# Keys of the context: from GpSimd operations to DMAs, in a two-layer cross-attention block

## The chip, the core and the metric

The kernel runs on one core of a Trainium2 chip. Its engines are TensorE (PE; PEld is its weight load), VectorE (DVE), ScalarE (ACT), GpSimd (POOL) and SyncE (SP, which here only issues DMAs). The metric is the device time of one execution in microseconds; the time before is 3352.13 us, the median of three runs (3349.53 to 3354.31).

## The reference

Two transformer blocks in float32, one after the other, over `x` of 4 x 512 x 320 and a context of 4 x 1601 x 192. There are 20 heads of 16.

```python
def _attn(x, ctx, wq, wk, wv, wo, bo, heads):
    q = (x @ wq).reshape(b, n, heads, dh).transpose(0, 2, 1, 3)
    k = (ctx @ wk).reshape(b, j, heads, dh).transpose(0, 2, 1, 3)
    v = (ctx @ wv).reshape(b, j, heads, dh).transpose(0, 2, 1, 3)
    a = softmax(einsum('bhid,bhjd->bhij', q, k) * dh ** -0.5)
    return einsum('bhij,bhjd->bhid', a, v).transpose(0, 2, 1, 3).reshape(b, n, -1) @ wo + bo
...
x = _attn(ln(x), ln(x), ...) + x            # self-attention
x = _attn(ln(x), context, ...) + x          # cross-attention, 1601 keys
a, g = split(ln(x) @ ff_w1 + ff_b1)
x = (a * gelu(g)) @ ff_w2 + ff_b2 + x       # feed-forward, 1280 wide
```

## The kernel before

**Units.** A layer is a list of units. A self-attention or cross-attention unit is one batch element and one group of four heads: 4 x 5 = 20 of each kind in a layer. A feed-forward unit is one batch element. Over two layers there are 40 cross units. A unit works through its keys in chunks of 128: 4 chunks in self-attention, 13 in cross-attention (12 full ones and a tail of 65 keys).

**What one chunk step does** (`main`, from L987). PE makes the scores of the chunk transposed, keys by queries, one matmul a head (`st`, L995). ACT takes their exponentials into `pr` (L1001). One step later PE multiplies these by the values of the four heads (`av`, L1015). Except for the first chunk, ACT copies that product to `vo` (L1031) and GpSimd adds it to the unit's sum `o` (L1032). `pr` and `vo` come from one ring of eight buffers (`prs`, L93, tag `pr`). Beside this, PE makes the scores of a coming unit a first time (`sps`, L835 and, for the tail, L849) and DVE takes their row maxima (`pm` and `nmax`, L843): the negated maximum goes into a row of the query tile by eight small DMAs (`max_end`, L885 to L899: `q<-turned`) three chunks before a unit ends, so that the score matmul subtracts it.

**Slots.** TensorE's rows are used in four slots of 32, a head in each. A head has 16 rows of keys, so half a slot is left: one row of it holds ones in the key tile, against the row of maxima in the query tile, and the others zeros. `HEAD` says which head a slot takes: slots 0 and 1 hold heads 0 and 2 in their lower 16 rows, slots 2 and 3 heads 1 and 3 in their upper 16. `keep` and `ones` are columns that mask the rows that a slot keeps and add its ones. The three key tiles `kT` (`kbuf`, L124) hold 128 rows by 1601 keys. Self units use `kbuf[0]`, three units beside each other; cross units use all three in turn. The feed-forward uses columns of `kbuf[1]` and `kbuf[2]` for its hidden values.

**Keys of the context** (`keys_of_context`, L687 to L721). The context stands transposed in four quarters of the array's rows, so each of four PSUM banks `a` takes a quarter of the keys, and in it each half `i` of the quarter has 64 rows: four heads of 16. The matmuls (L697) are 192 columns wide, with up to 32 more in half 1 for the tail, `more = [32, 32, 1, 0]`. ACT and DVE copy two banks each to a stage tile `kst` (L707), the columns of the tail by copies of their own (L709). Then eight closures (`piece`) are put on the unit's `kslots`; each calls `to_slots` (L572 to L587), which writes 64 rows of keys to both halves of the slots on GpSimd, two operations a piece for 192 keys and two more where there are tail columns:

```python
nc.gpsimd.tensor_scalar(to, stage[rows, :w], keep[b][rows], more[rows], ALU.mult, ALU.add)
```

Queries and the keys of self-attention go to their slots by the same line.

**What sets the order.** The instructions of each engine and each queue run in the order in which this program issues them. That order is planned while the program is built. There are chains of jobs (`divide`, `project`, `slots`, `norm`, `context`, `early`, `proj`, `values`), each job with a cost and a due round. `steps` (L360) runs once in a chunk step and takes the jobs with the nearest due round, as far as a credit allows; two rounds pass in a chunk step. Pieces cost 0.0, and `clock["slots"]` bounds them to two a step. When the last piece of a unit is issued, `there()` notes the round, and the first scores of that unit (`sps`) wait three rounds more (`at_hand`, L1201), unless they are due at once (`at_once`, L1205).

**Queues.** Nearly all DMAs go by SP, in the program's order: `q<-turned`, four `aT<-o` a unit that gather the finished output of a group (`turn` in `add_finish`, L926 to L934), the context loads (`load_context`, L492; two in flight, the next one issued by the job that has turned the last but one, which waits until three rounds after its load), weights, and the result. Weight loads wait in the list `loads`; one entry is issued in each attention unit, three chunks before its end. The rows behind the last tokens of the context, in its last tile of 128, are cleared by a memset on GpSimd (L503).

**Other work of GpSimd**: the residual's bias add (L465), part of the inverse root of the norms (L399 to L406), and the queries' slots.

Of the kernel before, what the change touches and what calls it, by code (L numbers as in the profile page):

```python
# [9 lines left out]
F32 = mybir.dt.float32  # L10
I32 = mybir.dt.int32
AF = mybir.ActivationFunctionType
ALU = mybir.AluOpType
# [4 lines left out]
S2, CTX = 1601, 192  # L18
H, DH = 20, 16
# [3 lines left out]
P = 128  # L23
NQ = N // P
G, HG = 5, 4
# [40 lines left out]
def kernel(ctx: ExitStack, tc: tile.TileContext, x, context, ws, out):  # L66
# [54 lines left out]
        nmax.append(m)  # L121


    kbuf = [const.tile([P, S2], F32, name=f"kT{i}") for i in range(3)]  # L124
    qbuf = [const.tile([P, N], F32, name=f"q{i}") for i in range(4)]
    fill = qbuf[3]
    nc.vector.memset(fill, 1.0)

    kept = []
    for b in range(2):  # L130
# [229 lines left out]
    def steps(beside, lights=1):  # L360


        tick()
        clock["lights"], clock["slots"] = lights, 2
        clock["tiles"] = True if beside is None else None
        done = 0
        while True:
            name = pick()
            if name is None:
                break  # L370
            cost = sum(chains[name][0][0])
            if cost >= 0.1:
                share = (0.5, 3.0) if beside else (9.0, 9.0) if beside is False else (0.5, 0.75, 1.5)
                least = cost * share[done] if done < len(share) else 3.0
                if clock["credit"] < (3.0 if beside is False else least):
                    break
                done += 1
                if clock["tiles"] is not None:
                    clock["tiles"] = name in ALIKE
            run(name)  # L380
            if cost == LIGHT:
                clock["lights"] -= 1
            clock["slots"] -= name == "slots"
        clock["tiles"] = None
# [107 lines left out]
    def load_context(b, i):  # L492
        c0, n = CGRP[i]
        t = two.tile([P, 2, CTX], F32, tag="ctxin", name="ctxin")
        rows = min(S2, (c0 + n) * P) - c0 * P
        full = rows // P
        if full:
            dma(
                out=t[:, :full, :],
                in_=context[b, c0 * P : (c0 + full) * P, :].rearrange("(c p) d -> p c d", p=P),  # L500
            )
        if rows % P:
            nc.gpsimd.memset(t[rows % P // SLOT * SLOT :, full, :], 0.0)  # L503
            dma(out=t[: rows % P, full, :], in_=context[b, (c0 + full) * P : S2, :])
        ctx_in[b, i] = t, clock["round"]

# [4 lines left out]
    def add_context(l, b, put, due, free):  # L511
        s = {}

        def tiles():
            s["cT"] = one.tile([P, KB, QT + 32], F32, tag="ctxT", name="ctxT")
            s["tail"] = one.tile([CK[0][2], 2, TAIL], F32, tag="tail", name="tail")

        def load():
            tiles()
            dma(out=s["cT"], in_=saved[b])  # L520
            dma(out=s["tail"], in_=saved_tail[b])
            s["round"] = clock["round"]

        if l:
            add("context", 0.0, load, due - 14, free)
            add("context", 0.0, lambda: put(s), due - 2, yes, lambda: clock["round"] >= s["round"] + 8)
            return

        def turn(i):
            if i == 0:  # L530
                tiles()
            c0, n = CGRP[i]
            t, _ = ctx_in.pop((b, i))
            for c in range(n):
                at = (c0 + c) * 32
                nc.vector.transpose(s["cT"][:, :, at : at + 32], t[:, c, :])
            if i + 2 < len(CGRP):
                load_context(b, i + 2)
            if i + 1 == len(CGRP):
                dma(out=saved[b], in_=s["cT"])  # L540
                s["last"] = t

        def tail():
            ps = step_bank([P, 2, P], "cps")
            for k, at, w in CK:
                nc.tensor.transpose(ps[:w, k, :TAIL], s["last"][:TAIL, 0, at : at + w], ident[:TAIL, :TAIL])
            w = CK[0][2]
            nc.scalar.copy(s["tail"], ps[:w, :, :TAIL])
            dma(out=saved_tail[b], in_=s["tail"])
            put(s)  # L550

        for i in range(len(CGRP)):
            add(
                "context", LIGHT, lambda i=i: turn(i), due - 2 * (len(CGRP) - i), free if i == 0 else yes,
                lambda i=i: clock["round"] >= ctx_in[b, i][1] + 3,
            )
        add("context", 0.3, tail, due)

# [13 lines left out]
    def to_slots(t, c0, stage, w, i, with_ones, direct=None):  # L572

        rows = slice(i * GD, (i + 1) * GD)
        for b in range(2):
            to = t[b * GD : (b + 1) * GD, c0 : c0 + w]
            more = ones[b] if with_ones else zero
            if direct:

                if b:  # L580
                    nc.vector.tensor_scalar(to, stage[rows, :w], direct[b][rows], more[rows], ALU.mult, ALU.add)
                else:
                    nc.scalar.activation(
                        to, stage[rows, :w], AF.Identity, bias=more[rows], scale=direct[b][rows]
                    )
                continue
            nc.gpsimd.tensor_scalar(to, stage[rows, :w], keep[b][rows], more[rows], ALU.mult, ALU.add)  # L587

    def add_proj(u):
# [97 lines left out]
        def keys_of_context():  # L687

            pss = quarter_banks("kps")

            more = [max(0, min(32, TAIL - a * 32)) for a in range(4)]
            for k in range(KB):
                for a, ps in enumerate(pss):
                    rows = slice(a * SLOT, (a + 1) * SLOT)
                    for i in range(2):
                        w = HALF + i * more[a]
                        nc.tensor.matmul(  # L697
                            ps[i * GD : (i + 1) * GD, :w],
                            lhsT=wk_q[rows, k, u.g * GD : (u.g + 1) * GD],
                            rhs=first.kvT[rows, k, i * HALF : i * HALF + w],  # L700
                            start=(k == 0),
                            stop=(k == KB - 1),
                        )
            stage = one.tile([P, 4, HALF + 32], F32, tag="kstage", name="kst4")
            for a, ps in enumerate(pss):
                copy = nc.vector.tensor_copy if a % 2 else nc.scalar.copy
                copy(stage[:, a, :HALF], ps[:, :HALF])  # L707
                if more[a]:
                    copy(stage[GD:, a, HALF : HALF + more[a]], ps[GD:, HALF : HALF + more[a]])  # L709
            for a in range(4):  # L710
                for i in range(2):
                    def piece(a=a, i=i):
                        to_slots(u.kT, a * QT + i * HALF, stage[:, a, :], HALF, i, True)
                        if i and more[a]:
                            to_slots(u.kT, 4 * QT + a * 32, stage[:, a, HALF:], more[a], i, True)
                        if a == 3 and i:
                            there()

                    u.kslots.append(piece)
            u.keyed = True  # L720
            first.made["kv"] += 1  # L721

# [14 lines left out]
        if not u.cross:  # L737
            add_queries()
            add(chain, (0.477,) * 3, keys, due, free)
        else:  # L740
            add(chain, 2.45, keys_of_context, keys_due, free)
            add_queries()
            for i in range(8):
                add(
                    "slots", 0.0, lambda: u.kslots and u.kslots.popleft()(), keys_due,
                    lambda: u.keyed, lambda: clock["slots"] > 0,
                )
# [434 lines left out]
    def after(u):  # L1182

        stage[u.b] += 1
        if u.b == B - 1:
            load_bias(u.l, ("self", "cross", "ff").index(u.kind) + 2)
            if u.kind == "self":
                loads.append(lambda: load_out(u.l, "o2_w"))
            if u.kind == "cross" and u.l + 1 < L:
                loads.append(lambda: load_out(u.l + 1, "o1_w"))  # L1190
            if u.l + 1 < L:
                if u.kind == "ff":
                    loads.append(lambda: load_cross(u.l + 1))
                    load_ff(u.l + 1)
                elif u.kind == "self":
                    loads.append(lambda: load_self(u.l + 1))
# [65 lines left out]
    load_bias(0, 0)  # L1262
    load_bias(0, 1)


    add_norms(0)
    add_proj(units[0])
    warm(5)
# [14 lines left out]
    max_reduce(first)  # L1283
    max_end(first)
    load_x(1)
    loads.append(lambda: load_x(2))
    loads.append(lambda: load_out(0, "o1_w"))
    loads.append(lambda: load_x(3))
    loads.append(lambda: load_cross(0))
# [51 lines left out]
```

## Time and profile before

| | |
|---|---|
| median of three runs | 3352.13 us |
| the profiled execution's own time | 3352.16 us |
| its span | 3350.4 us |
| mean granted clock of TensorE | 0.988 |
| L587, keys and queries to slots on GpSimd | 1036 + 476 operations |
| SP's DMAs on the hardware queue | 52416 packets, 52.15 MB |

The profile is one execution on the chip. Its span runs from the first to the last instruction. A row of a group gives the source line, engine and operation, what is written and read, the shape, the count, the busy time in us, the mean of one in ns, and the idle time of the engine just before these instructions with what ended it. In the view of waits a row reads "who <- for whom: us in total, times, longest us". In the timeline a row gives the start, the time it took, the engine and line, what it did, how many instructions are merged, and in brackets the idle time before. PE records two matmul instructions for one float32 matmul of the source. The page's stretches by time show the stages: self-attention of layer 0 up to about 325 us, its cross-attention to about 1400, feed-forward to about 1640, then the same for layer 1 up to the end at 3350.

| stretch, us | PE busy | DVE busy | ACT busy | POOL busy | granted clock |
|---|---|---|---|---|---|
| 0 to 320 | 310.20 | 240.46 | 196.89 | 169.04 | 1.00 |
| 320 to 1400 | 1041.01 | 787.58 | 752.81 | 616.18 | 0.97 |
| 1400 to 1640 | 239.25 | 61.30 | 43.98 | 27.67 | 1.00 |
| 1640 to 2000 | 353.24 | 234.21 | 198.04 | 161.27 | 1.00 |
| 2000 to 3030 | 1002.20 | 764.08 | 726.99 | 604.17 | 0.99 |
| 3030 to 3350 | 316.87 | 78.15 | 70.39 | 30.62 | 1.00 |

### The profile page before, as it was taken

What the parts mean: (1) busy time and instruction counts of PE and PEld (TensorE: products, weight loads), DVE (VectorE), ACT (ScalarE), POOL (GpSimd) and SP (SyncE); (2) the same over time, 40 slices, a digit from 0 to 9 for tenths busy, and PEclk for the clock granted to TensorE, in tenths of its full rate; (3) what the DMA queues carried; (4) which work ended last, traced back from release to release, by engine and by line L of the source; (5) the groups of instructions that cost most, each with busy time, mean ns of one, the idle gap of its engine ahead of it and who ended that gap; (6) DMA issues with size and microseconds to landing.
All of it is one profiled execution on the core that took longest, in us unless ns stands there. A gap on an engine that the chain in (4) does not pass through costs nothing.

```text
span 3350.4 us, 83401 instructions
## 1 busy us (share of the span) xinstructions
PE 3262.8 (97%) x33970; PEld 1506.1 (45%) x33970; DVE 2165.8 (65%) x4112; ACT 1989.1 (59%) x4031; POOL 1608.9 (48%) x2498
## 2 busy tenths in 40 slices
PE   9999999999999999999999999999999999999999
PEld 4444444444444444355444444444444444443555
DVE  7777776677777777622247777777777777774221
ACT  4666467677677677711136664677777777676110
POOL 4556455655656655211225564566556656642000
PEclk9999999999999999999999999999999999999999
DMA  1300001000000000100012000000000000000000
GB/s 50 82 20 25 7 14 33 21 9 12 24 9 10 26 4 5 39 1 1 1 31 48 25 10 7 9 24 5 5 19 5 5 20 5 5 5 36 9 10 14
DMA packets 52884, 57.49 MB, mean 17 GB/s; under 512 B 23693, under 2 KB 45589, under 8 KB 50965
## 3 DMA queue, kind: packets, MB, share of 16 engines
q1 hardware_dynamic: 52416, 52.15, 5.7%
q8 instruction: 268, 4.39, 0.6%
q14 instruction: 116, 0.94, 0.1%
q0 software_dynamic: 64, 0.00, 0.0%
q10 hardware_dynamic: 20, 0.00, 0.0%
HBM read 33.04 MB, written 7.93 MB: 12 GB/s over the span
## 4 chain that ended last, share of the span: by engine, by line
PE 80%; POOL 9%; DVE 5%; issue 2%; ACT 2%; SPq 1%; DMA 1%; POOLq 0%; DVEq 0%; ACTq 0%
PE st L995 21%; PE av L1015 16%; PE sps L835 11%; PE fps L1118 8%; PE yps L1153 5%; POOL kT L587 4%; POOL o L1032 3%; PE ops L943 3%; PE kps L697 3%; PE vps L788 3%; PE qps L639 2%; PE fps L1130 2%; DVE nmax L843 2%; DVE pm L843 2%; POOL q L587 1%
## 5 line engine op out<-in xcount | busy, mean ns | idle before, releaser
L1001 ACT ACTIVATE pr<-st 128x512 f32<-128x512 f32 (+1 forms) x2720 | 1424.9, 602 | 567.3 <-PE sps L835 308.5
L995 PE MATMUL st<-q,kT 32*128 32x512 f32 (+1 forms) x5440 | 1421.8, 620 | 56.2 <-ACT pr L1001 42.8
L843 DVE TENSOR_REDUCE pm<-sps 128x1 f32<-128x512 f32 x1920 | 1196.9, 682 | 318.9 <-PE sps L835 314.6
L835 PE MATMUL sps<-kT,q 32*128 32x512 f32 x5120 | 1351.1, 627 | 14.9 <-POOL kT L587 9.3
L1032 POOL TENSOR_TENSOR o<-o,vo 128x512 f32<-128x512 f32 x576 | 735.0, 1276 | 998.4 <-ACT vo L1031 900.3
L995 PEld LDWEIGHTS st<-q,kT 32*128 32x128 f32 (+1 forms) x5440 | 525.4, 181 | 599.2 <-ACT pr L1001 365.5
L1015 PE MATMUL av<-pr,vals 128*32 128x512 f32 (+1 forms) x5440 | 742.6, 615 | 2.0 <-ACT pr L1001 2.0
L587 POOL TENSOR_SCALAR kT<-kst,keep,ones 64x192 f32<-64x192 f32 (+3 forms) x1036 | 496.0, 479 | 158.1 <-ACT kst L707 64.7
L835 PEld LDWEIGHTS sps<-kT,q 32*128 32x128 f32 x5120 | 446.9, 185 | 127.8 <-issue 57.1
L843 DVE TENSOR_REDUCE nmax<-sps 128x1 f32<-128x512 f32 x640 | 396.0, 680 | 150.2 <-PE sps L835 149.1
L1031 ACT COPY vo<-av 128x512 f32<-128x512 f32 x576 | 344.1, 597 | 44.0 <-PE av L1015 42.7
L1015 PEld LDWEIGHTS av<-pr,vals 128*32 128x32 f32 (+1 forms) x5440 | 110.6, 109 | 504.5 <-ACT pr L1001 475.6
L1118 PE MATMUL fps<-hT,w 128*128 128x512 f32 x640 | 288.0, 599 | 0.0
L1136 ACT ACTIVATE gl<-fps,b 128x512 f32<-128x512 f32 x80 | 54.8, 687 | 376.6 <-PE fps L1130 376.6
L587 POOL TENSOR_SCALAR q<-qst,keep,zero 64x128 f32<-64x128 f32 (+1 forms) x476 | 230.3, 484 | 52.0 <-ACT qst L651 15.5
L1118 PEld LDWEIGHTS fps<-hT,w 128*128 128x128 f32 x640 | 117.4, 190 | 147.1 <-issue 140.9
L400 POOL TENSOR_SCALAR root<-root 128x4 f32<-128x4 f32 x23 | 5.3, 230 | 297.3 <-DVE root L394 296.7
L1137 DVE SCALAR_TENSOR_TENSOR hid<-fps,b,gl 128x512 f32<-128x512 f32 x48 | 35.8, 750 | 153.0 <-ACT gl L1136 150.6
L639 PE MATMUL qps<-hT,wq 112*32 112x128 f32 (+3 forms) x2880 | 129.1, 315 | 2.8 <-DVE nmax L843 2.4
L943 PEld LDWEIGHTS ops<-wo,aT 112*32 112x32 f32 (+1 forms) x3072 | 98.1, 110 | 67.5 <-issue 52.7
L639 PEld LDWEIGHTS qps<-hT,wq 112*32 112x32 f32 (+1 forms) x2880 | 87.5, 113 | 90.7 <-issue 47.6
L465 POOL TENSOR_TENSOR x<-x,brow 128x320 f32<-128x320 f32 x96 | 83.4, 886 | 91.4 <-DVE hn L439 79.3
(88 smaller groups left out, 2265.6 us busy)
## 6 DMA issues: line engine op xcount, KB each, us to landing
aT<-o SPq DMA_DIRECT2D x320, 32.0 KB
q<-turned SPq DMA_DIRECT2D x636, 1.0 KB
ctxT<-ctxT SPq DMA_DIRECT2D x8, 1248.0 KB
w<-in_L_xattn_ff_w_dram SPq DMA_DIRECT2D x4, 1280.0 KB
ctxin<-in_ctx_dram SPq DMA_DIRECT2D x24, 192.0 KB
w<-in_L_xattn_ff_w_dram SPq DMA_DIRECT2D x4, 800.0 KB
out_dram<-x SPq DMA_DIRECT2D x16, 160.0 KB
x<-in_x_dram SPq DMA_DIRECT2D x3, 640.0 KB
```

Of the source, the lines that this page charges most:

```text
L587: nc.gpsimd.tensor_scalar(to, stage[rows, :w], keep[b][rows], more[rows], ALU.mult, ALU.add)
L639: nc.tensor.matmul(ps[to, :w], lhsT=wq[:n, k, gs], rhs=first.hT[:n, k, at[i] : at[i] + w], start=(k == 0), stop=(k == 2),)
L835: nc.tensor.matmul(ps, lhsT=u.q[j * SLOT : (j + 1) * SLOT, t * P : (t + 1) * P], rhs=u.kT[j * SLOT : (j + 1) * SLOT, u.k0 + s * 512 : u.k0 ...
L843: return lambda: nc.vector.tensor_reduce(to, ps, AX.X, ALU.max, negate=(ns == 1))
L943: nc.tensor.matmul(ps[f : f + m, : D // 2], lhsT=aT[:n, k, t * P + f : t * P + f + m], rhs=wo[:n, k, cols], start=(k == 0), stop=(k == 2),)
L995: nc.tensor.matmul(st[:r, :], lhsT=u.kT[rows, u.k0 + u.cols[c] : u.k0 + u.cols[c] + r], rhs=u.q[rows, :], start=True, stop=True)
L1001: nc.scalar.activation(p[:r], st[:r], AF.Exp)
L1015: nc.tensor.matmul(ps[i * SLOT : (i + 1) * SLOT, :], lhsT=columns_of[:r, head : head + SLOT], rhs=pr.pop((c, j))[:r, :], start=True, stop= ...
L1031: nc.scalar.copy(vo, ps)
L1032: nc.gpsimd.tensor_tensor(u.o, u.o, vo, ALU.add)
L1118: nc.tensor.matmul(ps, lhsT=w1[:, k, i * FF + c * P : i * FF + (c + 1) * P], rhs=u.hT[:, k, :], start=(k == 0), stop=False,)
L1153: nc.tensor.matmul(ps[:, :D], lhsT=hid[c][:, t * P : (t + 1) * P], rhs=w2[:, c, :], start=(c == 0), stop=(c == NHC - 1),)
```

## The change

The keys of the context are written to their slots by DMAs on SP. A slot's 16 key rows are filled for all quarters at once: two DMAs of 16 rows by 4 runs of 192 keys, one for each half, and one of 16 rows by 4 runs of 32 for the tail. A unit has four pieces, one a slot, with three DMAs each, and a step takes one piece. The rows of zeros and ones are no longer written with the keys: `rows_of_ones` writes them on GpSimd, at the start for the columns of `kbuf[0]` behind those that self units write, in the second and third unit for the other two tiles (through `loads`, which moves later loads back by two units), and again after the feed-forward of layer 0, which has overwritten parts of both. So that a DMA has four equal runs, the matmuls of all banks and halves are 224 columns wide, the stage copies too, and the key tiles get 1664 columns. The rows behind the last tokens are cleared on VectorE. The jobs that turn the context wait four rounds after their load instead of three.

```diff
-    kbuf = [const.tile([P, S2], F32, name=f"kT{i}") for i in range(3)]
+    kbuf = [const.tile([P, 4 * QT + P], F32, name=f"kT{i}") for i in range(3)]
...
+    def rows_of_ones(k, new=True):
+        if new:
+            nc.gpsimd.memset(k, 0.0)
+        for b in range(2):
+            rows = slice(b * GD, (b + 1) * GD)
+            nc.gpsimd.tensor_scalar(k[rows], k[rows], zero[rows], ones[b][rows], ALU.mult, ALU.add)
...
-        clock["lights"], clock["slots"] = lights, 2
+        clock["lights"], clock["slots"] = lights, 1
...
-            nc.gpsimd.memset(t[rows % P // SLOT * SLOT :, full, :], 0.0)
+            nc.vector.memset(t[rows % P // SLOT * SLOT :, full, :], 0.0)
...
-                lambda i=i: clock["round"] >= ctx_in[b, i][1] + 3,
+                lambda i=i: clock["round"] >= ctx_in[b, i][1] + 4,
...
-            more = [max(0, min(32, TAIL - a * 32)) for a in range(4)]
...
-                        w = HALF + i * more[a]
+                        w = HALF + 32
...
-                copy(stage[:, a, :HALF], ps[:, :HALF])
-                if more[a]:
-                    copy(stage[GD:, a, HALF : HALF + more[a]], ps[GD:, HALF : HALF + more[a]])
-            for a in range(4):
-                for i in range(2):
-                    def piece(a=a, i=i):
-                        to_slots(u.kT, a * QT + i * HALF, stage[:, a, :], HALF, i, True)
-                        if i and more[a]:
-                            to_slots(u.kT, 4 * QT + a * 32, stage[:, a, HALF:], more[a], i, True)
-                        if a == 3 and i:
-                            there()
-                    u.kslots.append(piece)
+                copy(stage[:, a, :], ps[:, : HALF + 32])
+            def piece(j):
+                to = u.kT[j * SLOT + DH * (j > 1) : j * SLOT + DH * (j > 1) + DH, :]
+                full = to[:, : 4 * QT].rearrange("d (a w) -> d a w", a=4)
                 for i in range(2):
+                    rows = slice(i * GD + HEAD[j] * DH, i * GD + (HEAD[j] + 1) * DH)
+                    dma(out=full[:, :, i * HALF : (i + 1) * HALF], in_=stage[rows, :, :HALF])
+                dma(out=to[:, 4 * QT :].rearrange("d (a w) -> d a w", a=4), in_=stage[rows, :, HALF:])
+                if j == HG - 1:
+                    there()
+            for j in range(HG):
+                u.kslots.append(lambda j=j: piece(j))
...
-            for i in range(8):
+            for _ in range(HG):
                 add("slots", 0.0, ...)
...
                 if u.kind == "ff":
+                    for k in kbuf[1:]:
+                        rows_of_ones(k, False)
...
-    loads.append(lambda: load_x(2))
+    rows_of_ones(kbuf[0][:, 4 * QT :])
+    for k in kbuf[1:]:
+        loads.append(lambda k=k: rows_of_ones(k))
+    loads.insert(0, lambda: load_x(2))
```

## The prediction

> **What bounds the kernel now.** First the page: busy times, chain, groups.
>
> ```profile
> PE 3262.8 (97%) x33970; PEld 1506.1 (45%) x33970; DVE 2165.8 (65%) x4112; ACT 1989.1 (59%) x4031; POOL 1608.9 (48%) x2498
> PE 80%; POOL 9%; DVE 5%; issue 2%; ACT 2%; SPq 1%; DMA 1%; POOLq 0%; DVEq 0%; ACTq 0%
> L587 POOL TENSOR_SCALAR kT<-kst,keep,ones 64x192 f32<-64x192 f32 (+3 forms) x1036 | 496.0, 479 | 158.1 <-ACT kst L707 64.7
> ```
>
> TensorE (PE) has the path, yet GpSimd (POOL), busy 48%, holds 9% of it. An engine half idle can only do that in bursts. The waits of ScalarE (ACT), then of PE:
>
> ```profile
> ACT pr L1001 <- POOL o L1032: 166.2, 117, 5.9
> PE st L995 <- ACT pr L1001: 42.8, 34, 2.7
> PE sps L835 <- POOL kT L587: 9.3, 2, 4.6
> ```
>
> 117 times an exponential (L1001) waited until GpSimd had added an output chunk (L1032): `pr` and `vo` share the ring `prs` of eight buffers, and a `vo` is free only after that add. The third view is the timeline of GpSimd in one cross unit, with one row of PE's:
>
> ```profile
> 948.99 3.23 POOL L587 TENSOR_SCALAR kT<-kst,keep,ones 64x192 f32<-64x192 f32 x6 [3.72 <-ACT kst L707]
> 953.94 3.15 POOL L587 TENSOR_SCALAR kT<-kst,keep,ones 64x192 f32<-64x192 f32 x6
> 957.17 1.27 POOL L1032 TENSOR_TENSOR o<-o,vo 128x512 f32<-128x512 f32 x1
> 965.21 2.06 POOL L587 TENSOR_SCALAR q<-qst,keep,zero 64x128 f32<-64x128 f32 x4
> ...
> 969.30 1.17 PE L995 MATMUL st<-q,kT 32*128 32x512 f32 x2 [2.06 <-ACT pr L1001]
> ```
>
> The key pieces and the adds run gapless from 952.7 to 968.6: the adds fall behind, ACT runs out of buffers, PE stands 2.06 us. Windows over that place show the clock afterwards (the column before DMA share and GB/s):
>
> ```profile
> 957.00:966.60 9.60, 9.60 (x108) 4.17 (x104) 6.81 (x12) 5.71 (x12) 8.51 (x16) 1.00 0.01 3
> 969.30:974.00 4.70, 4.70 (x40) 1.98 (x40) 1.29 (x2) 3.09 (x6) 1.42 (x2) 0.64 0.00 0
> ```
>
> PE's idle time understates this, since PE also runs thin before it stops. I cut PE's timeline at each start of an `av` group (L1015) and compared stretches in which PE does the same work. The commonest (8 st, 8 sps, 8 av records; 250 of them) takes 2.92 us at least, 2.93 in the median, 3.35 in the mean. Summing what each stretch takes above the fastest of its make-up gives 91.6 us in the cross stage of layer 0 and 73.3 in that of layer 1. Of these 164.9 us, 114.4 lie in stretches in which a `pr` or `vo` waits for GpSimd. Another 10.1 lie in seven stretches after such a stall, without such a wait but at half clock (717.8, 971.1, 1223.4, 2385.0, 2581.7, 2632.3, 2879.1 us). So 124.5 us hang on GpSimd's backlog. The rest is not: some 9 us near 580 us is VectorE waiting for context, and about 31 us are half-microsecond hitches.
>
> **The parts of the change, costed.**
>
> *Removed from GpSimd*: per cross unit 16 operations of 64x192 (503 ns), 4 of 64x32 (372), 2 of 64x1 (346): 10.2 us, over 40 units 409 us of 1608.9. What remains in a unit is 12 adds of 1.276 us, 8 query operations of 0.448 and a few small ones, about 20 us in a unit of some 50. The worst close pair, one add and four queries (1.27 + 2.06 = 3.33 us), exceeds one 2.93 us step by 0.4, which eight buffers take up. I credit 90% of 124.5: **-112**. Bounds: -60, if other bursts (queries, the residual add L465 at 886 ns) keep half, and -124.5.
>
> Here a rule speaks for less. The Trainium skill (TensorE: Matmul & The Clock Gate, Part 1) has the clock fall to half after at least one idle window of about 3.4 us. By it only the two 4.63 us stalls (333, 2014 us) would give clock back, and the 10.1 would not be in the sum: 0.9 x 114.4 = 103. In the trace the clock fell to a mean of 0.64 after a stall of 2.06 us. I keep the row.
>
> *Added on the sync queue (SP)*: 12 DMAs per unit, four of them 8 KB, eight 48 KB. No row has this shape. The nearest:
>
> ```profile
> 953.31 2.46 SPq L934 DMA_DIRECT2D aT<-o  x4
> ```
>
> 0.615 us to issue one of 32 KB from SBUF to SBUF. Lower bound 0.50 (q<-turned), upper 1.1 (w1r, 1.109 in the median, also 64 rows). I take 0.615: 12 x 0.615 = 7.4 us, and 2.9 us to land (the only landing the page gives, q<-turned), so keys lie ready 10.3 us after the stage copies; at 1.1 it is 16.1. The first reader comes after four steps, one piece each, and three rounds more (two rounds a step): 5.5 steps x 2.93 = 16.1 us. Lateness 0 to 0; today's pieces end some 16 us after (948.99 to 965.1). The skill speaks against this (DMA: Bandwidth & Descriptors, Anatomy of one DMA; its rules call transfers under 64 KB mostly overhead): about 2 us fixed per DMA. Paid in series that is 24 us, 8 late, 38 x 8 = 300 us lost. But the row shows four DMAs within 2.46 us, so the fixed part overlaps. I keep the row: **0**.
>
> What is queued behind on SP: aT<-o (read no sooner than three rounds later, and only after a batch's fifth unit), the context loads, and q<-turned. From SP's timeline, in 38 of 40 units the next q<-turned is 29 us or more after the key projection; 7.4 us of issuing is over by then. In the two early units it is 6.2 and 9.1 us; delay at most 1.6 us. There the two 4.63 us waits for POOL kT end as well; keys would be there near 324 us where PE stopped at 328.8. SP's new wait, for the stage copies, is over when PE has done the projection just ahead in program order. **0 to +6, taken 1.**
>
> *The projection*: all eight matmuls of a k step become 224 wide; today five are 192, one 193, two 224, and the group takes 2.43 us on the chain. vps L788 takes 2.16 us for six steps of 192 columns and 1.55 of 128, 1.6 ns a column and step: 224 would give 2.47. So the widest already sets the pace: 0 to +0.1 us a unit, **+2**.
>
> *Stage copies*: ACT loses 168-ns copies (two a unit), its main two grow from 319 to about 345 ns (256 columns take 372): 0.97 to 0.69 us. DVE loses one of 194. PE felt this: the step after a projection took 0.31 us longer, as ACT copied until 949.60. Gain 0 to 0.3 a unit, taken 0.2 x 40: **-8**.
>
> *Zeros and ones*: nearest rows are TENSOR_SCALAR at 346 ns (1 column), 503 (192), 557 (256), so 0.83 ns a column: 1.73 us for 1664; the memset of 4435 columns took 3.793, so 1.43 for 1664. Layer 0: two buffers, each 1.43 + 2 x 1.73 = 4.9 us, in the second and third self unit, where GpSimd is a bit over half busy (169 of 320 us): bounds 0 and +10, taken **+3**. kbuf[0]'s tail: about 1.1 us at the start, hidden before the first scores. End of layer 0's feed-forward: 4 x 1.73 = 6.9 us when GpSimd has only small operations waiting; 0 to +7, taken **+2**.
>
> *VectorE's memset*: GpSimd's took 0.27 us, four times; nothing either way (0 to +1). Loads shifted by two units: o1_w is issued at 70.1 us, first used at 148.6; two units are 30 us, hidden. Context turns at four rounds instead of three: steps lie two rounds apart, so 3 already rounds up to 4: 0.
>
> *Waits on PE*: pieces arrive on several DMA semaphores. An event-semaphore row on PEld is 51 ns; up to 8 more a unit, 0 to +16 us, mostly under running matmuls (PEld is 45% busy): **+4**.
>
> *What is late next*: VectorE does four maxima in 2.48 us of a 2.93 us step, and its odd jobs (divide 0.41, transposes 0.7) no longer fall into stalls. Today's half-microsecond hitches cost 31 us in stretches without backlog; 0 to +20, taken **+6**.
>
> Sum: -112 + 1 + 2 - 8 + 3 + 2 + 4 + 6 = -102. The profiled execution took 3352.16 us (span 3350.4, 1.8 around it), 0.03 off the median of 3352.13. Forecast **3250 us** (-3.0%).
>
> **Rivals.**
> *Half the gain* (0.15): ACT or VectorE becomes the limit as soon as GpSimd's queue is gone. For it: VectorE's 2.48 of 2.93. Against: the undisturbed stretches already run at 2.92 with both. -60 - 4 + 15 = about -50: 3302.
> *All of the gain* (0.10): backlog gone wholly, hitches too: -124.5 - 11 + 5: about 3222.
> *It doesn't do what it says* (0.03): the adds themselves, 1.27 us each, hold the ring, and the waits persist; near 3350. Against: outside the bursts they wait for ACT (L1032 idles 998 us).
> *Slower, keys late on SP* (0.05): if a strided DMA costs SP 1.6 us (the longest aT<-o issue was 1.604), keys come 12 x 1.6 + 2.9 = 22.1 us after, 6 late; PE then waits in 38 units, 228 us, less the 102: about 3478. It decides from (16.1 - 2.9 + 102/38)/12 = 1.3 us an issue.
> The forecast itself: 0.67.
>
> **Numbers.** Range 3225 to 3305: it takes in the half gain, most of the largest, and leaves out the last two. A measurement tells this kernel from no change at about 0.2%. Faster 0.92, same 0.03, slower 0.05.
>
> **What would show it.** Right: exponentials' waits for POOL o fall from 166 us to below 30; PE st's wait for ACT pr from 42.8 to below 12; POOL near 1215 us busy; fewer half-clock windows, mean clock above 0.99; kps groups near 2.45 us; the commonest stretch at a mean near 3.0. Wrong: waits of PE for DMA kT, q<-turned landing late, new SP issues over 1.1 us, or maxima (L843) as the main releaser of PE.

## The result and the profile after

The changed kernel takes 3269.05 us (median of four runs, 3267.90 to 3272.27) against 3352.88 for the kernel before (the three runs of before and a fourth): a ratio of 0.9753, 95% interval 0.9736 to 0.9770. That is 83.8 us less; the forecast was 102 less. In the profiled execution the span is 3266.6 us and the mean clock 0.996, against 3350.4 and 0.988.

Lines of the page that answer to those of before (source lines lie 7 to 9 further down now):

```profile
PE 3209.3 (98%) x33970; PEld 1495.2 (46%) x33970; DVE 2170.3 (66%) x4076; ACT 1973.4 (60%) x3951; POOL 1219.4 (37%) x1627
```

GpSimd lost 389.5 us of work, as costed (-409 for the keys, +18 for zeros and ones). PE is 53.5 us less *busy* with the same number of instructions. About half of that is the clock: time at half clock (granted clock 0.5) fell from 81.9 to 27.3 us, and there a score matmul is counted as busy for up to 1162 ns instead of 587. The other half is not taken apart. The waits of ACT, and those of PE:

```profile
ACT pr L1010 <- POOL o L1041: 29.6, 30, 4.3
```

```profile
PE ops L952 <- DMA aT<-o: 9.0, 1, 9.0
PE st L1004 <- DVE nmax L852: 6.3, 10, 0.7
PE sps L844 <- DVE pm L852: 6.3, 1, 6.3
PE st L1004 <- ACT pr L1010: 6.1, 8, 1.0
```

The exponentials' wait for GpSimd fell from 166.2 us in 117 places to 29.6 in 30. PE's wait for the exponentials fell from 42.8 to 6.1, and the two 4.63 us waits for POOL kT are gone. At the top stands a wait that was not there before: an output projection waits 9 us for its input DMA.

SP with the new pieces, in the timeline of one cross unit:

```profile
689.76 1.38 SPq L722 DMA_DIRECT2D kT<-kst  x2
691.23 0.58 SPq L723 DMA_DIRECT2D kT<-kst  x1
...
693.88 2.46 SPq L943 DMA_DIRECT2D aT<-o  x4
```

A DMA of the keys takes 0.612 us to issue in the median (L722), the tail's 0.585: the row taken for them, aT<-o, was near. The projection on PE:

```profile
729.49 2.53 PE L704 MATMUL kps<-ctxT,w 32*64 32x224 f32 x96
```

2.50 us before, 2.53 now with all matmuls at 224 columns: the widest did set the pace.

The same stretches between `av` groups that the prediction used give the account by stage, in us above the undisturbed pace:

| | before | after |
|---|---|---|
| cross stages, an exponential or `vo` waits for GpSimd | 114.4 | 8.0 |
| cross stages, half clock without such a wait | 18.8 | 9.8 |
| cross stages, other | 31.6 | 57.4 |
| self stage of layer 0 | 9.3 | 24.3 |
| self stage of layer 1 | 8.5 | 9.0 |

In the clock row, 10.1 us of before were the backlog's and are gone; the rest belongs to one stall on the context near 580 us, in both kernels. A stretch with a projection also got shorter at its undisturbed pace, from 5.72 to 5.43 us.

### The profile page after: what moved, and what is told of

Read it like the earlier page. It is cut to its first block, busy times and chain, and to the rows that moved or that the text cites. A ratio compares the mean times of both kernels' runs of the same rounds, so it can differ in the third digit from the quotient of the medians.

```text
span 3266.6 us, 83246 instructions
## 1 busy us (share of the span) xinstructions
PE 3209.3 (98%) x33970; PEld 1495.2 (46%) x33970; DVE 2170.3 (66%) x4076; ACT 1973.4 (60%) x3951; POOL 1219.4 (37%) x1627
## 4 chain that ended last, share of the span: by engine, by line
PE 61%; DVE 4%; POOL 1%; DMA 0%; issue 0%; ACT 0%; SPq 0%; DVEq 0%; POOLq 0%
PE st L1004 14%; PE av L1024 12%; PE fps L1127 9%; PE sps L844 9%; PE yps L1162 5%; PE fps L1139 2%; PE ops L952 2%; PE kps L704 2%; PE qps L648 2%; PE vps L797 2%; DVE pm L852 1%; DVE nmax L852 1%; PE sps L858 1%; PE hps L461 1%; PE kps L674 1%; PE vps L779 1%
## 5 line engine op out<-in xcount | busy, mean ns | idle before, releaser
L1004 PE MATMUL st<-q,kT 32*128 32x512 f32 (+1 forms) x5440 | 1377.7, 615 | 19.0 <-DVE nmax L852 6.3
L852 DVE TENSOR_REDUCE pm<-sps 128x1 f32<-128x512 f32 x1920 | 1191.7, 681 | 241.2 <-PE sps L844 237.3
L844 PE MATMUL sps<-kT,q 32*128 32x512 f32 x5120 | 1326.2, 621 | 11.5 <-DVE pm L852 6.3
L1004 PEld LDWEIGHTS st<-q,kT 32*128 32x128 f32 (+1 forms) x5440 | 511.4, 181 | 509.8 <-ACT pr L1010 295.1
L1024 PE MATMUL av<-pr,vals 128*32 128x512 f32 (+1 forms) x5440 | 729.8, 605 | 2.0 <-ACT pr L1010 2.0
L844 PEld LDWEIGHTS sps<-kT,q 32*128 32x128 f32 x5120 | 453.9, 184 | 146.8 <-issue 73.7
L852 DVE TENSOR_REDUCE nmax<-sps 128x1 f32<-128x512 f32 x640 | 395.6, 680 | 134.6 <-PE sps L844 133.4
L596 POOL TENSOR_SCALAR q<-qst,keep,zero 64x128 f32<-64x128 f32 (+1 forms) x476 | 231.8, 487 | 50.0 <-ACT qst L660 16.1
L952 PE MATMUL ops<-wo,aT 112*32 112x160 f32 (+1 forms) x3072 | 127.4, 302 | 9.0 <-DMA aT<-o 9.0
```

Of the source, the lines that this page charges most:

```text
L844: nc.tensor.matmul(ps, lhsT=u.q[j * SLOT : (j + 1) * SLOT, t * P : (t + 1) * P], rhs=u.kT[j * SLOT : (j + 1) * SLOT, u.k0 + s * 512 : u.k0 ...
L852: return lambda: nc.vector.tensor_reduce(to, ps, AX.X, ALU.max, negate=(ns == 1))
L952: nc.tensor.matmul(ps[f : f + m, : D // 2], lhsT=aT[:n, k, t * P + f : t * P + f + m], rhs=wo[:n, k, cols], start=(k == 0), stop=(k == 2),)
L1004: nc.tensor.matmul(st[:r, :], lhsT=u.kT[rows, u.k0 + u.cols[c] : u.k0 + u.cols[c] + r], rhs=u.q[rows, :], start=True, stop=True)
L1024: nc.tensor.matmul(ps[i * SLOT : (i + 1) * SLOT, :], lhsT=columns_of[:r, head : head + SLOT], rhs=pr.pop((c, j))[:r, :], start=True, stop= ...
```

## The experiments

Each ratio is to runs of the kernel before made beside that run. Differences in us between two runs are those of their medians; read from the ratios they come out within 4 us of that.

**The burst put back beside the DMAs.**

```diff
+    dump = const.tile([P, HALF + 32], F32, name="dump")
...
                 dma(out=to[:, 4 * QT :].rearrange(...), in_=stage[rows, :, HALF:])
+                more = max(0, min(32, TAIL - j * 32))
+                for i in range(2):
+                    to_slots(dump, 0, stage[:, j, :], HALF, i, True)
+                    if i and more:
+                        to_slots(dump, HALF, stage[:, j, HALF:], more, i, True)
```

> The changed kernel, with the 22 GpSimd operations of a cross unit put back beside the DMAs, at their old places, writing the same shapes to a tile that nobody reads. Theory (the gain is GpSimd's backlog gone): the stalls come back; 3335 to 3370 us, exponentials' waits for POOL o back above 120 us from 0 in the list of the long ones. Rival (the gain is the DMA route itself: keys earlier, narrower bursts of copies): within 15 us of the changed kernel's 3269.

3370.45 us, ratio 1.0058 (1.0044 to 1.0071), at the upper end of what was expected: 101 us above the changed kernel. Its waits of ACT for GpSimd:

```profile
ACT pr L1016 <- POOL o L1047: 184.3, 122, 6.3
```

The same 880 operations, now useless, bring 122 waits and 119.6 us of stretches with them. So GpSimd's occupation is the cost, and not how or when keys arrive. The DMA route by itself gives no more than room on GpSimd. That this run is some 20 us slower than the kernel before goes for the most part with the self stage of layer 0, which is as long here as in the changed kernel (24 us above the undisturbed pace against 9.3); its cause comes below.

**Only the wide projection and the single copies, in the kernel before.**

```diff
-                        w = HALF + i * more[a]
+                        w = HALF + 32
...
-                copy(stage[:, a, :HALF], ps[:, :HALF])
-                if more[a]:
-                    copy(stage[GD:, a, HALF : HALF + more[a]], ps[GD:, HALF : HALF + more[a]])
+                copy(stage[:, a, :], ps[:, : HALF + 32])
```

> The kernel before with only the 224-column projection and the single stage copies; keys still go to their slots on GpSimd. Theory: the stretch with a projection falls from 5.72 to about 5.43 us as in the changed kernel, but the backlog behind it begins 0.3 us earlier and takes part of it back: 3342 to 3352 us. Rival (copies and widths carry the gain): below 3320.

3346.33 us, 0.9985 (0.9976 to 0.9994). Inside the expected range: the stretch with a projection falls from 5.72 to 5.45 us, and about 5 us come of the 11 that the shorter stretches are worth. The edit is a small part of the gain.

**Where the zeros and ones are written.** At the very start, with the old order of loads:

```diff
     nc.vector.memset(zero, 0.0)
+    rows_of_ones(kbuf[0][:, 4 * QT :])
+    for k in kbuf[1:]:
+        rows_of_ones(k)
...
```

> The changed kernel, zeros and ones written at the very start, where GpSimd stands idle for 9.5 us, and the loads in their old order. Theory (the two-unit shift of the loads made the output DMA of a group wait behind the cross weights, 9 us of PE idle at 163 us, and the long operations cost GpSimd in the third self unit): self stage of layer 0 back to its old length, 3253 to 3258 us. Rival (the 9 us are SP's own slowness or the aT DMAs): 3266 to 3270.

Behind the other loads ("rows last" from here on):

```diff
...
     load_ff(0)
+    for k in kbuf[1:]:
+        loads.append(lambda k=k: rows_of_ones(k))
```

> The changed kernel, with the rows of zeros and ones of two tiles put behind the other loads (eighth and ninth unit) instead of in front of them, so that only the order of the loads is undone and GpSimd still does the same long operations. Theory: the 9 us stall at 163 us and its half clock go, 10 to 12 us; a few us of GpSimd stall stay in another unit: 3256 to 3261 us. Rival (GpSimd's long operations, not the loads, cost the self stage): 3265 to 3270.

The second took 3254.48 us, 0.9713 (0.9700 to 0.9727): 15 us better than the changed kernel, a little more than expected. The first took 3264.36, 0.9740 (0.9727 to 0.9753), short of what was expected. It also lost the stall at 163 us, and got another at the start:

```profile
17.54 0.82 PE L464 MATMUL hps<-ident,hn 128*112 128x128 f32 x2 [8.42 <-DVE hn L451]
```

VectorE's timeline there shows why. First the changed kernel, then the same operations in this run, whose lines lie 3 further down, and last GpSimd in this run:

```profile
6.08 0.17 DVE L404 TENSOR_SCALAR root<-root 128x4 int32<-128x4 int32 x1
...
6.49 0.16 DVE L412 TENSOR_TENSOR root<-root 128x4 f32<-128x4 f32 x1
...
6.88 0.17 DVE L414 TENSOR_SCALAR root<-root 128x4 f32<-128x4 f32 x1
```

```profile
6.45 1.51 DVE L407 TENSOR_SCALAR root<-root 128x4 int32<-128x4 int32 x1
...
8.19 1.57 DVE L415 TENSOR_TENSOR root<-root 128x4 f32<-128x4 f32 x1
...
10.00 1.61 DVE L417 TENSOR_SCALAR root<-root 128x4 f32<-128x4 f32 x1
```

```profile
6.45 1.48 POOL L132 MEMSET kT<- 128x1664 f32 x1
8.03 3.55 POOL L135 TENSOR_SCALAR kT<-kT,zero,ones 64x1664 f32<-64x1664 f32 x2
```

These operations of 0.17 us take 1.5 to 1.6 when they start under one of GpSimd's long operations. "GpSimd is idle there" was true, and not enough: VectorE worked on the path beside it.

**The margin on SP**, each half's DMA in two, then in four:

```diff
-                    dma(out=full[:, :, i * HALF : (i + 1) * HALF], in_=stage[rows, :, :HALF])
+                    for a in range(0, 4, 2):    # range(4) and a + 1 for 36
+                        dma(out=full[:, a : a + 2, i * HALF : (i + 1) * HALF], in_=stage[rows, a : a + 2, :HALF])
```

> The changed kernel, each half's DMA split in two: 20 DMAs a cross unit instead of 12. By the prediction's sum keys lie ready 20 x 0.61 + 2.9 = 15.1 us after the stage copies, just inside the 16.1 us that the program leaves: 3266 to 3280 us. Rival (SP is already short): over 3290.

> The changed kernel, each half's DMA split in four: 36 DMAs a cross unit. By the prediction's slower rival keys come 36 x 0.5 to 0.61 + 2.9 = 20.9 to 24.9 us after the copies, 5 to 9 us late in 38 units: 3450 to 3600 us, with waits of PE for DMA kT. Rival (the first reader comes later than 16.1 us, or SP's issues run beside other waits): below 3320.

20 DMAs: 3268.93 us, 0.9756 (0.9740 to 0.9772), no loss. 36 DMAs: 3329.58, 0.9940 (0.9925 to 0.9955), some 60 us lost, between the two expectations, and by another way than the one named:

```profile
PE ops L953 <- DMA aT<-o: 40.6, 9, 9.3
PE st L1005 <- DMA q<-turned: 8.6, 8, 2.8
```

One of the nine waits for aT<-o, 9.3 us, is the one that the changed kernel has too. Both kinds together grow from 10.6 us to 49.2, and time at half clock from 27.3 us to 81.9.

No wait of PE for DMA kT is in the list, though the last key DMA of a unit was typically issued some 27 us after the projection. The first reader of the keys comes later than the 16.1 us of the prediction's sum: in the changed kernel a cross unit's first `sps` starts 21.0 us or more after the stage copies, 27.4 in the median. With 36 DMAs it starts in 17 of the 40 units even before the last key DMA is issued; the first chunk lies in the first quarter, whose DMAs are separate now. So this run does not show what late keys would cost. What suffers is what queues behind them on SP.

**Hitches of VectorE**, the half-microsecond and longer stops in the row "other", on the kernel with rows last. The divide of a finished group goes to GpSimd, its transpose back one step later:

```diff
         def divide():
-            nc.vector.tensor_tensor(
+            nc.gpsimd.tensor_tensor(
                 turned[:, :, :DH], turned[:, :, :DH], ...
             )
+            when.append(clock["round"])
+
+        def back():
             nc.vector.transpose(u.o, turned.rearrange("p b s -> p (b s)"))
             when.append(clock["round"])
...
+        add("divide", LIGHT, back, r - 20, yes, since(2, 1))
-        add("divide", 0.0, turn, r - 20, lambda: u.g or held["open"] < 2, since(2, 1))
+        add("divide", 0.0, turn, r - 20, lambda: u.g or held["open"] < 2, since(3, 1))
```

> The changed kernel with the loads in their old order (rows of ones behind them), and the divide of a finished group on GpSimd, with its transpose back one step later, so that VectorE never works with two SBUF inputs while GpSimd adds. Theory (34 of 80 divides there began under a GpSimd operation and took up to 1.6 us instead of 0.42, which pushed the maxima late): the stretches that are 1.5 to 1.7 us over go, 3230 to 3245 us; the kernel with the load order alone had 3254. Rival (hitches come from VectorE's load as such, transposes and residual adds): 3250 to 3256.

3205.85 us, 0.9568 (0.9554 to 0.9582): more than expected. The edit did two things, so one more run kept the divide on VectorE:

> As the run with the divide on GpSimd, but the divide stays on VectorE; only the transpose back comes one step later. It parts the two things which that edit did at once. Theory (the collisions cost, since VectorE's divide still begins under GpSimd's adds): 3235 to 3254 us, most of the 49 us stays lost. Rival (it was the bunching of divide and transpose in one step): 3203 to 3215 us.

3214.37 us, 0.9584 (0.9571 to 0.9598). The rival was right about the time. The divide still began under GpSimd's operations, 35 of 80 over 0.7 us, and yet nearly all of the gain came: room in the step is enough. The timeline in the changed kernel shows what stood there before, VectorE first and then GpSimd:

```profile
736.49 2.41 DVE L852 TENSOR_REDUCE pm<-sps 128x1 f32<-128x512 f32 x4
738.82 1.43 DVE L928 TENSOR_TENSOR oturn<-oturn,rd 128x256 f32<-128x256 f32 x1
740.28 0.71 DVE L932 STREAM_TRANSPOSE o<-oturn 128x512 f32<-128x512 f32 x1
740.92 0.28 DVE L959 TENSOR_TENSOR x<-ops,x 128x160 f32<-128x160 f32 x1
```

```profile
738.70 1.26 POOL L1041 TENSOR_TENSOR o<-o,vo 128x512 f32<-128x512 f32 x1 [7.03 <-ACT vo L1040]
```

Four maxima, a divide, a transpose and a residual add make 4.8 us, in a step of PE of 3.75 us (2.93 and a projection of 0.82). But 1.0 us of the 4.8 is the collision: the divide takes 1.43 us, where 0.42 is its median. And where the divide was not slowed, the bunching cost little. In the changed kernel the stretch with a divide and the one after it lose 38.7 us in all in the 35 places where it was slowed, and 10.5 us in the 43 others. Among pairs of stretches in which PE makes no projection at all it is 1.77 us against 0.44 in the median (9 and 15 places). So by the trace both make the hitch: a slowed divide, in a step too full to bear it. The later transpose gives the step room for it; to take away the collision alone was not tried.

The other stretches of the cross stages fall from 57.4 us to 27.8, about the 31.6 of before, and the two self stages by some 10 us together against the kernel with rows last. What the divide on GpSimd adds beyond that lies inside the overlap of the two intervals and stays open.

**The same edit in the kernel before.**

> The kernel before with only the divide on GpSimd and its transpose one step later; keys still go to their slots on GpSimd. Theory (VectorE and GpSimd collide there too, but the key burst dominates and the divide makes it longer): 3325 to 3355 us, far less than the 49 us that the same edit gave behind the change. Rival (the divide's collisions are independent of the keys): 3300 to 3312.

3353.29 us, 0.9993 (0.9984 to 1.0002): nothing. The other stretches shrink from 31.6 to 17 us there too, but those with waits for GpSimd grow from 114.4 to 130.1. The edit itself puts 80 divides of some 0.6 us on GpSimd, so this run does not tell what the hitch was worth in the kernel before; the later transpose alone was not run there.

**Context turns six rounds after their load**, on the kernel with rows last. The stall that it aims at stands so in the changed kernel:

```profile
589.20 0.64 DVE L545 STREAM_TRANSPOSE ctxT<-ctxin 128x192 f32<-128x192 f32 x2 [7.28 <-DMA ctxin<-in_ctx_dram]
```

VectorE waits for the context's tile, and PE for the maxima behind it (the 6.3 us of `sps` above). The edit:

```diff
-                lambda i=i: clock["round"] >= ctx_in[b, i][1] + 4,
+                lambda i=i: clock["round"] >= ctx_in[b, i][1] + 6,
```

> The changed kernel with the loads in their old order, and context turns six rounds after their load instead of four. Theory (the 6 us stall of PE near 580 us is VectorE waiting in order for a context tile whose DMA stood behind 23 others on SP): stall and its half clock go, 3243 to 3248 us against 3254. Rival (turns are forced later when the keys fall due, the stall moves): 3252 to 3262.

3239.85 us, 0.9669 (0.9655 to 0.9683), a little better than expected. Gone are the wait of 6.1 us near 570 us (where the stall stands with rows last), two of 1.2 us for context tiles later in that stage, and the half clock behind all three (10.2 us and twice 3.4): 15 us in all.

**The two small edits undone**: the memset back on GpSimd, three rounds instead of four.

> The changed kernel with the memset of the context's last rows back on GpSimd and context turns three rounds after their load. The prediction costed both at nothing: 3265 to 3273 us against 3269. Rival (turns at three rounds stand longer on the context's DMA, or the clear hurts VectorE): over 4 us either way.

3268.06 us, 0.9744 (0.9728 to 0.9760): nothing for the two together, as costed.

**The gains together**: rows last, divide on GpSimd with the later transpose, six rounds.

> The changed kernel with three more edits: loads in their old order, the divide on GpSimd with its transpose one step later, context turns six rounds after their load. Theory: the last two act at different places and add up; the stall near 570 us and its half clock (about 12 us) go from 3206: 3191 to 3197 us. Rival: without the collisions VectorE reaches the context later or earlier, the stall has another length: 3198 to 3207.

3194.01 us, 0.9522 (0.9508 to 0.9537), the fastest kernel of the study, 2.3% under the changed one.

## Why the prediction was right, and where its sum was off

*The mechanism* was as told. Putting the burst back cost 101 us; the term was -112. In the stretches it is 106.4 and the 10.1 at half clock, -116.5. Here the row was the better guide than the rule of one idle window: stalls of about 2 us did bring half clock, though not every one, and without the stalls the windows went. Sixteen stretches at half clock lie inside the span before and five after, one of these following the 6.3 us wait and one the 9 us wait.

Of the signs that it named, most came: 29.6 us of waits for POOL o, 6.1 for ACT pr, 1219 us of GpSimd, a clock of 0.996. The commonest stretch stayed at a mean of 3.13 us, not 3.0. And one sign named for being wrong came true: the maxima (L852) are now what PE waits for most, 22.6 us in all. They stood at 20.8 before, so the larger waits went and these were left.

*Projection and copies*: +2 and -8 predicted; the stretch with a projection is 0.29 us shorter, about -11 over the units. Right in sign; the run with these two edits alone shows nearly the same stretch, 5.45 us.

*Zeros and ones, with the loads*: +3, +2 and 0 predicted, some +15 measured, nearly all in the self stage of layer 0. The step that failed is the sentence on the loads shifted by two units. It asked whether the moved load (`o1_w`) is still early enough, and it is. It did not ask what the *other* loads of that list meet at their new place. The cross weights now go out just when the first batch's fifth unit sends its output:

```profile
139.75 4.45 SPq L905 DMA_DIRECT2D q<-turned  x8
...
150.46 1.88 SPq L219 DMA_DIRECT2D w<-in_L_xattn_k_dram  x4
152.38 1.89 SPq L219 DMA_DIRECT2D w<-in_L_xattn_v_dram  x4
154.38 3.51 SPq L943 DMA_DIRECT2D aT<-o  x4
```

PE wanted that output in the middle of the projection and got it 9 us later:

```profile
162.90 3.83 PE L952 MATMUL ops<-wo,aT 96*32 96x160 f32 x56 [8.96 <-DMA aT<-o]
```

Before, the same weights went out at 105 to 115 us and pushed only an aT<-o that nobody was waiting for yet. Undoing the order alone gave 15 us back, with GpSimd's long operations still there. The operations' own times were right (1.764 us measured for 1.73, 1.486 for 1.43); the +3 for them is not seen when they lie in later units.

*What is late next*: +6 predicted, +26 measured (31.6 to 57.4). Named rightly as VectorE's odd jobs, sized too small: they were counted one by one and at their undisturbed times against the 0.45 us that VectorE has free in a step. Not counted were those that the plan puts into the *same* step, and the slowing of the divide by GpSimd's adds, which struck 20 of 80 divides before the change and 35 after it. This term and the one before are the missing 30 us; against them stand about 10 us better in the first two terms and the 5 us of SP and of the waits that did not show. That the sum came within 18 us is in part this offsetting.

*Keys on SP*: 0.612 us an issue against 0.615 taken. The about 2 us for each DMA that the prediction set against this stand in the Trainium skill (DMA: Bandwidth & Descriptors, Anatomy of one DMA) for DMAs that GpSimd issues; here SP issued them, and no wait for them is seen.

*The slower rival*: its sum was far off. With 36 DMAs it should have lost 180 us or more and lost 60, since its 16.1 us to the first reader are 21 or more. Keys were never late; aT<-o, which the prediction dismissed as read no sooner than three rounds later, is what SP's time comes out of.

*Waits on PE* (+4) could not be told apart from nothing; no run isolates them. The traces show 813 semaphore instructions on PE where there were 757, 56 more and not 320 (the 8 a unit of the prediction's upper bound): at the prediction's 51 ns each, under 3 us.

## What to carry to other kernels

An engine at 48% can set the time if its work comes in bursts in front of a small ring of buffers: read who waits for it, in time order, and cost the whole train, with the clock that follows. When work is freed from one engine or a list of loads is shifted, look at every entry that moves, and at what each meets on its new place in the queue. The next limit is found in the fullest single step of the next engine, with its operations at the times that they take beside the other engines, not in its mean load.

## What the runs showed of the hardware that was not expected

VectorE operations on SBUF can stretch to the end of a GpSimd operation that is under way: 0.17 us became 1.51 to 1.61 beside GpSimd's 1.48 to 1.8 us operations, and the divide of 0.42 us up to 1.59 us beside its adds. Not every one did: beside the second memset of that run (11.64 to 13.12 us) two TENSOR_TENSOR of 128x4 kept 0.16 us, and the TENSOR_SCALAR after them took 0.92. Maxima that read PSUM kept their 0.68 us throughout. The Trainium skill (GPSIMD Engine Reference, Specifications) says that the two engines share interfaces and names VectorE's two-port modes and two SBUF inputs. The divide, with two SBUF inputs, agrees; in which mode the TENSOR_SCALAR of one input ran, these traces don't show. The wait lasted for up to the whole of the other's operation. It cost 8 us where VectorE was alone on the path (the rows written at the start), about 1.3 us a time where VectorE's step was already full, and little where it had a step's room.
